# A two-layer graph network on one core: degrees turned on TensorE, four counted groups for five in layer 1, and a split by upper halves

## The chip, the cores and the metric

The kernel runs on one core of a Trainium2 chip. The metric is the device time of one execution in microseconds. A core has TensorE (PE, with its weight loads PEld), VectorE (DVE), ScalarE (ACT), GpSimd (POOL) and SyncE (SP). Each of them takes its instructions in order; they meet through semaphores. SP issues nearly all plain transfers here, POOL all gathers of rows.

## The reference

There are 12500 nodes with 256 features each, and 200000 edges, sorted by destination. `dst` is 12500 u², so that low nodes have many edges and high ones few.

```python
def _sage_conv(x, src, dst, W_l, b_l, W_r):
    msgs = x[src]
    agg = segment_sum(msgs, dst)
    deg = segment_sum(ones, dst)
    mean = agg / maximum(deg, 1.0)[:, None]
    return mean @ W_l + b_l + x @ W_r

h = relu(_sage_conv(x, src, dst, W1_l, b1, W1_r))
h = relu(_sage_conv(h, src, dst, W2_l, b2, W2_r))
out = layernorm(x + h @ W3 + b3)
```

## The kernel before, in words

**Two ways to a sum.** The edges lie in 1563 tiles of 128, the nodes in NB = 98 blocks of 128. The sums over edges are formed in one of two ways.

*Gathered.* For a tile of edges POOL gathers 128 rows of the table by an indirect DMA (`got`, L251), four tiles a round, into one of four buffers `got`. DVE makes one-hot tiles (`one` L208, `two` L214), PE multiplies each tile's rows into a strip of 32 destinations (`part_ps`, L263), ACT copies (`some`, L273), PE spreads the strips over 128 destinations (`sum_ps`, L279), and DVE adds them to a ring of eight blocks in SBUF (`sums`, L293). In layer 1 a column of ones gives the degree too (L285, added to the row `degs` at L289). POOL may start a round when the strips of four rounds ago are done.

*Counted.* For the lowest destinations, in groups of DN = 256, there is no gather. A matrix of counts (source by destination) is made by one-hot products: `pick` (DVE, L680), `low` and `aft` (DVE, L684 and L690), `count_ps` (PE, L723 and L727), copied by ACT into `counts` (L729). Then one product per group, over all 98 blocks of x, gives the sums (`dense_ps`, L655): x stands in HBM as three bf16 parts whose sum is x (`x3_d`), and its rows are loaded two blocks at a time (`rows`, L649, four buffers). In layer 1 the degrees of a counted group come from 196 products with a column of ones (L744). The first HG1 = 5 groups are counted in layer 1, HG = 7 in layer 2. Layer 2's table is h in the same three parts (`h3_d`). A group counted in layer 1 is stored to `count_d` (L778) and loaded again in layer 2; the last two counted in layer 1 simply stay in the two buffers `counts`.

`lows[g]` is the first tile that may hold a destination of group g, for g = 0 to 7: 0, 208, 304, 376, 432, 488, 536, 576. Gathers of layer 1 start at `lows[HG1]`, those of layer 2 at `lows[HG]`.

**Parts.** `exact` (L629) makes the three parts: ACT rounds to bf16, DVE subtracts, ACT rounds the rest, DVE subtracts. It runs for the 98 blocks of x (`split_rows`, in layer 1's first stage) and for the 98 blocks of h (`first_block`).

**Blocks.** When a block's sums are complete, `first_block` (L907) in layer 1, in three pieces, loads the block's rows of x, transposes them (`transposed`, L852: PE L855 into a bank of four 128-column places, ACT's copy L857 to `own_t`), and multiplies sums and rows by the weights (`sage`, L874). A mean needs the reciprocal of the degree of each node as a column (`rdeg`), while the ring holds degrees as a row of one partition (`degs`). Before, the row is stored to HBM (`deg_d`, L913) and read back as a column (L918); DVE then does the max and the reciprocal (L922, L923). `last_block` does layer 2's, in five pieces, with the last weights and the layer norm.

**What sets the order.** The order on PE and POOL is written out by hand; DVE, ACT and SP get theirs from a scheduler, in order of expected readiness. `layer` (L576) runs over the rounds of gathers: each round is one `gathers.step()`, then up to three pieces of blocks, and between these counted work from a generator. How much counted work stands in a round is set by cost: `due = dense_cost * min(1, (i + 1 - i0) / (n - i0 - 8))`, so all of it is spread evenly over the rounds of the layer, less the last eight. The costs are estimates written in the kernel (`COST_DENSE`, `count_cost` and so on), and `mixed` interleaves parts of a stage. `stages_1` gives the stages of layer 1: stage 0 counts group 0 and splits x; each later stage multiplies group g - 1, counts group g and stores. `stages_2` does the same for layer 2. By these formulas, layer 1 has 269 rounds (eight of them in the set-up), and its stages, in rounds, take 57, 40, 41, 37, 41 and 38; layer 2 has 247 rounds, and its stages take 31, 51 and five times 31.

Of the kernel before, what the change touches and what calls it, by code (L numbers as in the profile page):

```python
# [7 lines left out]
F32 = mybir.dt.float32  # L8
F16 = mybir.dt.float16
BF16 = mybir.dt.bfloat16  # L10
# [3 lines left out]
OP = mybir.AluOpType  # L14
# [9 lines left out]
P = 128  # L24
# [25 lines left out]
def by_runs(  # L50
# [27 lines left out]
    nc = tc.nc  # L78
    N, D = x.shape
    E = src.shape[0]  # L80
    NB = -(-N // P)
    NC = D // P
# [14 lines left out]
    def at_most(t):  # L97
        return N * ((t + SLACK) / NT) ** 2 + 2

    HG1, HG, DN = 5, 7, 256
    lows = [max(t for t in range(0, NT, 2 * G) if t == 0 or at_most(t) < DN * g) for g in range(HG + 1)]
    highs = [min(t for t in range(0, NT, G) if at_least(t) >= DN * (g + 1)) for g in range(HG)]
    HT = highs[-1]
# [21 lines left out]
    dram = ctx.enter_context(tc.tile_pool(name="dram", bufs=1, space=DRAM))  # L127
# [1 line left out]
    x3_d = dram.tile([P, NB, 3, D], BF16, name="x3_d")  # L129
    h3_d = dram.tile([P, NB, 3, D], BF16, name="h3_d")  # L130
    count_d = dram.tile([HG1 - 1, P, NB, DN], BF16, name="count_d")
    deg_d = dram.tile([NB, P], F32, name="deg_d")


    src_t = consts.tile([P, (CH - C0) * P], I32, name="src_t")
# [14 lines left out]
    ones = consts.tile([P, 1], F32, name="ones")  # L150
# [144 lines left out]
    with tc.tile_pool(name="setup", bufs=1) as su, \  # L295
# [163 lines left out]
        start = su.tile([P, HC], F32, name="start")  # L459
# [8 lines left out]
        for g, (c0, c1) in enumerate(spans):  # L468
            n = c1 - c0
# [46 lines left out]
        for t in range(0, HT, 32):  # L516
            n = min(32, HT - t)
# [52 lines left out]
    work = ctx.enter_context(tc.tile_pool(name="work", bufs=2))  # L570
# [57 lines left out]

    def exact(t, s, rest):  # L629

        nc.scalar.copy(s[:, 0], t)
        nc.vector.tensor_tensor(rest, t, s[:, 0], op=OP.subtract)
        nc.scalar.copy(s[:, 1], rest)
        nc.vector.tensor_tensor(s[:, 2], rest, s[:, 1], op=OP.subtract)

    def split_rows(b):
        t = load_rows(x, N, b, "split_sb")
        s = work.tile([P, 3, D], BF16, name="parts")
        exact(t, s, t)
        nc.sync.dma_start(x3_d[:, b], s)  # L640

    def product(g, table3, c_sb):
# [116 lines left out]
    def counting(g):  # L759
        return sum(count_cost(t) for t in range(lows[g], highs[g]))  # L760
# [20 lines left out]
    def loaded(g, c_sb):  # L781
        for b0 in range(0, NB, 14):
            nc.sync.dma_start(c_sb[:, b0:b0 + 14, :DN], count_d[g, :, b0:b0 + 14])
            yield 0.5

    def dense(g, table3, c_sb, waiting, with_deg):
        for p in product(g, table3, c_sb):
            if isinstance(p, float):
                yield p
            else:  # L790
                d_sb = p
        if with_deg:
            yield from degrees(g, c_sb)
        for j in range(DN // P):
            waiting.append((g * (DN // P) + j, d_sb[:, :, j * P:(j + 1) * P]))

    def splits():
        for b in range(NB):
            split_rows(b)
            yield COST_SPLIT  # L800
# [1 line left out]
    D_1 = NB * COST_DENSE + DN // P * (NB // 14) * COST_DEGREES  # L802
    D_2 = NB * COST_DENSE
    MOVED = NB // 14 * 0.5
    assert NB % 14 == 0 and HG == HG1 + 2

    def stages_1(waiting):

# [9 lines left out]

    def stages_2(waiting):

        order = [HG1 - 1, HG1, HG1 + 1, *range(HG1 - 1)]
        for i, g in enumerate(order):
            parts = [(dense(g, h3_d, counts[(HG1 - 1 + i) % 2], waiting, False), D_2)]
            if 1 <= i < HG - 1:
                n = order[i + 1]
                to = counts[(HG1 + i) % 2]
                parts.append((count(n, to), counting(n)) if n > HG1 else (loaded(n, to), MOVED))
            yield parts
# [15 lines left out]
    def load_rows(table, n_rows, b, name, tag=None):  # L844
        t = work.tile([P, D], F32, name=name, tag=tag or name)
        n = min(P, n_rows - b * P)
        if n < P:
            nc.vector.memset(t, 0.0)
        nc.sync.dma_start(t[:n], table[b * P:b * P + n, :])
        return t  # L850

    def transposed(t, ps, name):  # L852

        for c in range(NC):
            nc.tensor.transpose(ps[:, c], t[:, c * P:(c + 1) * P], ident)  # L855
        s = work.tile([P, NC, P], F32, name=name)
        copied = nc.scalar.copy(s, ps[:, :NC])  # L857
        return s, copied.ins.name

    def ring(b):  # L860

        r = (b % RB) * P
        return sums[:, :, r:r + P], degs[:, r:r + P]
# [10 lines left out]
    def sage(own_t, copied, b, agg, of_ring, wl, wr, bias, name):  # L874

        ps = block_bank()
        for c in range(NC):
            product = nc.tensor.matmul(ps[:, 0], lhsT=agg[:, c], rhs=wl[:, c], start=c == 0,  # L878
                                       stop=c == NC - 1)
            if c == 0:  # L880
                tc.add_manual_dep(product.ins, copied, LANDED, reason="the other products' rows")
        for c in range(NC):
            product = nc.tensor.matmul(ps[:, 1], lhsT=own_t[:, c], rhs=wr[:, c], start=c == 0,  # L883
                                       stop=c == NC - 1)
        if of_ring:
            zeroed = nc.scalar.copy(agg, zeros)  # L886
            tc.add_manual_dep(zeroed.ins, product.ins.name, LANDED, reason="it signals for all")
        own = work.tile([P, D], F32, name="own")
        nc.vector.tensor_add(own, ps[:, 1], bias)  # L889
        nc.vector.scalar_tensor_tensor(own, ps[:, 0], rdeg[:, b:b + 1], own, op0=OP.mult, op1=OP.add)  # L890
        h = work.tile([P, D], F32, name=name)
        nc.scalar.activation(h, own, AF.Relu)  # L892
        return h, own

    def block_bank():

        if block_pool is None:
            t = mixed_pool.tile([P, 4, P], F32, name="block_ps", tag="mixed")
        else:
            t = block_pool.tile([P, 4, P], F32, name="block_ps")  # L900
        return t.rearrange("p (two a) l -> p two (a l)", two=2)

    def turned():
        t = block_bank()
        return t.rearrange("p two (a l) -> p (two a) l", l=P)

    def first_block(b, agg=None):  # L907
        x_sb = load_rows(x, N, b, "x_sb")
        of_ring = agg is None
        if of_ring:  # L910
            overlap(b, True)
            agg, deg_row = ring(b)
            nc.sync.dma_start(deg_d[b:b + 1], deg_row)  # L913
        yield True
        if of_ring:
            deg = work.tile([P, 1], F32, name="deg")
            with nc.allow_non_contiguous_dma(reason="a row becomes a column"):
                nc.sync.dma_start(deg, deg_d[b, :, None])  # L918
        x_t, copied = transposed(x_sb, turned(), "own_t")
        yield True  # L920
        if of_ring:
            nc.vector.tensor_scalar(deg, deg, 1.0, None, op0=OP.max)  # L922
            nc.vector.reciprocal(rdeg[:, b:b + 1], deg)  # L923
        h, own = sage(x_t, copied, b, agg, of_ring, w1l_sb, w1r_sb, biases[:, 0], "h")
        if of_ring:
            nc.scalar.copy(deg_row, zeros[0:1, 0])
        nc.sync.dma_start(h_d[b * P:(b + 1) * P, :], h)
        s = work.tile([P, 3, D], BF16, name="parts")
        exact(h, s, own)
        nc.sync.dma_start(h3_d[:, b], s)  # L930
        yield True

    def last_block(b, agg=None):
        h_sb = load_rows(h_d, NB * P, b, "h_sb", "split_sb")
        of_ring = agg is None
        yield True
        if of_ring:
            overlap(b, False)
            agg, _ = ring(b)
        h_t, copied = transposed(h_sb, turned(), "own_t")  # L940
        yield True
        h2, _ = sage(h_t, copied, b, agg, of_ring, w2l_sb, w2r_sb, biases[:, 1], "h")
        x_sb = load_rows(x, N, b, "x_sb")
        yield True
        h2_t, _ = transposed(h2, turned(), "own_t")
        nc.vector.tensor_add(x_sb, x_sb, biases[:, 2])
        yield True
        y = block_bank()
        for c in range(NC):
            nc.tensor.matmul(y[:, 0], lhsT=h2_t[:, c], rhs=w3_sb[:, c], start=c == 0, stop=c == NC - 1)  # L950
        z = work.tile([P, D], F32, name="z", tag="own")
        nc.vector.tensor_add(z, y[:, 0], x_sb)
        stats = work.tile([P, 6], F32, name="stats")
        nc.vector.bn_stats(stats, z)
        mv = work.tile([P, 2], F32, name="mv")
        nc.vector.bn_aggr(mv, stats)
        std = work.tile([P, 1], F32, name="std")
        nc.scalar.activation(std, mv[:, 1:2], AF.Sqrt, bias=eps)
        rstd = work.tile([P, 1], F32, name="rstd")
        nc.vector.reciprocal(rstd, std)  # L960
        nc.vector.tensor_scalar(z, z, mv[:, 0:1], rstd, op0=OP.subtract, op1=OP.mult)
        n = min(P, N - b * P)
        nc.sync.dma_start(out[b * P:b * P + n, :], z[:n])
        yield True
# [386 lines left out]
```

## Time and profile before

| what | value |
|---|---|
| median of three runs | 2878.88 us (2876.56 to 2884.81) |
| the profiled execution's own time | 2859.28 us |
| its span, first to last instruction | 2857.5 us |
| mean granted TensorE clock | 0.918 |
| first gather starts, last gather of layer 1 ends | 24.8 us, 1532.8 us |
| first gather of layer 2 starts, last ends | 1556.8 us, 2804.6 us |
| gathers in layers 1 and 2 | 1076, 988 |
| layer 1's products by group, first matmul | 421.5, 667.7, 883.0, 1077.2, 1298.4 us |

The page gives, for each engine, the busy time, the share of the span and the number of instructions; then the span in 40 slices, a digit a slice; then the chain that ended last; then groups of instructions as "line, engine, operation, out<-in, count | busy, mean ns of one | idle before, and what ended it". Names have their numbers left out, so `h_d` stands for `h3_d` too and `x_d` for `x3_d`. "issue" is idle time in which the engine waited for nothing that the profile shows. A matmul with fp32 operands appears as two records.

### The profile page before, as it was taken

To read this page: it belongs to the slowest core of one execution; us is meant where nothing else is said; L and a number is where in the kernel's file an instruction comes from. 1 tells how busy PE (TensorE), PEld (TensorE's weight loads), DVE (VectorE), ACT (ScalarE), POOL (GpSimd) and SP (SyncE) were. 2 spreads that over 40 slices of the span, in tenths; PEclk is the share of its full clock that TensorE was granted. 3 is DMA by queue.
4 is the path that set the end of the run, shared out by engine and by line. 5 is a ranking of instruction groups with operands and counts; after the bars stand their busy time and mean duration, and the time that the engine had idled before them with its cause. 6 is when DMAs were issued, how large, how long until landed. Compare 5 with 4: busy or idle time off the path is not lost.

```text
span 2857.5 us, 53445 instructions
## 1 busy us (share of the span) xinstructions
PE 2325.8 (81%) x18268; PEld 1607.4 (56%) x18268; DVE 1461.6 (51%) x4334; ACT 1099.4 (38%) x2270; POOL 2054.2 (72%) x2074
## 2 busy tenths in 40 slices
PE   3466675888988998999996678777889889999995
PEld 1122333565755666766664455555656667777773
DVE  6688774654555565565564124443324344444443
ACT  0422774654554564565563013333112122222222
POOL 5777775677777777777675777777777777777771
PEclk9876877997998999999997999999999999999998
DMA  4466679778878879877764777777989999888872
GB/s 124 135 180 179 190 210 300 248 225 257 267 224 254 291 219 297 262 215 228 247 212 132 229 244 231 222 225 226 294 285 306 295 301 309 283 264 270 271 248 70
DMA packets 420975, 676.49 MB, mean 237 GB/s; under 512 B 72420, under 2 KB 279386, under 8 KB 420698
## 3 DMA queue, kind: packets, MB, share of 16 engines
q1 hardware_dynamic: 316263, 400.60, 43.5%
q0 software_dynamic: 99072, 270.66, 31.3%
q8 instruction: 150, 2.46, 0.4%
q10 hardware_dynamic: 5362, 1.72, 0.3%
q14 instruction: 128, 1.04, 0.1%
HBM read 582.84 MB, written 89.92 MB: 235 GB/s over the span
## 4 chain that ended last, share of the span: by engine, by line
PE 45%; DMA 24%; POOL 11%; issue 8%; DVE 7%; ACT 4%; SPq 1%; DVEq 0%; ACTq 0%; POOLq 0%
PE dense_ps L655 17%; POOL got L251 11%; PE part_ps L263 6%; PE block_ps L878 5%; DMA got<-h_d,src_t 4%; DMA rows<-h_d 4%; PE block_ps L883 4%; PE count_ps L723 4%; DMA x_sb<-in_x_dram 4%; PE sum_ps L279 4%; DMA rows<-x_d 4%; DMA split_sb<-in_x_dram 3%; DMA got<-in_x_dram,src_t 2%; PE block_ps L950 2%; PE block_ps L855 2%
## 5 line engine op out<-in xcount | busy, mean ns | idle before, releaser
L251 POOL DMA_INDIRECT got<-in_x_dram,src_t x1076 | 1109.7, 1031 | 420.3 <-issue 282.7
L251 POOL DMA_INDIRECT got<-h_d,src_t x988 | 942.4, 954 | 329.4 <-issue 260.8
L655 PE MATMUL dense_ps<-counts,rows 128*128 128x256 bf16 x7056 | 958.4, 279 | 75.4 <-DMA rows<-h_d 41.1
L655 PEld LDWEIGHTS <-rows 128*128 128x128 bf16 x7056 | 674.2, 99 | 296.7 <-issue 81.4
L729 ACT CAST counts<-count_ps 128x686 f32 (+2 forms) x620 | 540.2, 872 | 237.8 <-PE count_ps L723 188.0
L263 PE MATMUL part_ps<-got,one 128*32 128x257 f32 (+1 forms) x4128 | 359.9, 422 | 181.9 <-DMA got<-h_d,src_t 106.1
L723 PE MATMUL count_ps<-pick,low 128*128 128x490 bf16 (+2 forms) x1052 | 321.1, 359 | 62.5 <-ACT counts L729 37.2
L680 DVE TENSOR_SCALAR pick<-steps,key_t 128x686 bf16<-128x686 f16 (+2 forms) x748 | 301.0, 414 | 120.9 <-PE count_ps L723 107.3
L208 DVE TENSOR_TENSOR one<-lo_t,lane_b 128x128 f32<-128x128 bf16 x516 | 148.1, 287 | 322.5 <-PE part_ps L263 318.8
L273 ACT COPY some<-part_ps 128x257 f32<-128x257 f32 (+1 forms) x361 | 134.5, 373 | 414.2 <-PE part_ps L263 413.1
L279 PE MATMUL sum_ps<-two,some 128*128 128x128 f32 x1444 | 240.9, 293 | 39.4 <-DVE own L890 38.6
L263 PEld LDWEIGHTS part_ps<-got,one 128*32 128x32 f32 x4128 | 87.2, 112 | 299.8 <-issue 237.9
L279 PEld LDWEIGHTS sum_ps<-two,some 128*128 128x128 f32 x1444 | 209.4, 205 | 55.3 <-DVE own L890 39.9
L293 DVE TENSOR_TENSOR sums<-sums,sum_ps 128x256 f32 x361 | 148.3, 411 | 145.8 <-PE sum_ps L279 113.2
L886 ACT COPY sums<-zero 128x256 f32<-128x256 f32 x172 | 69.3, 403 | 393.4 <-PE block_ps L883 391.8
L889 DVE TENSOR_TENSOR own<-block_ps,biases 128x256 f32<-128x256 f32 x196 | 82.6, 421 | 210.3 <-PE block_ps L883 209.9
L723 PEld LDWEIGHTS <-low 128*128 128x128 bf16 x1052 | 105.0, 101 | 140.0 <-DVE pick L680 33.6
L857 ACT COPY own_t<-block_ps 128x256 f32<-128x256 f32 x294 | 108.8, 372 | 125.6 <-PE block_ps L855 124.5
L684 DVE TENSOR_TENSOR low<-low_t,lane_b 128x512 bf16<-128x512 bf16 x187 | 127.7, 683 | 39.4 <-PE count_ps L727 39.0
L892 ACT ACTIVATE h<-own 128x256 f32<-128x256 f32 x196 | 81.7, 417 | 145.3 <-DVE own L890 145.0
L727 PE MATMUL count_ps<-aft,low 128*128 128x98 bf16 x614 | 133.3, 217 | 0.0
L878 PE MATMUL block_ps<-w1l_sb,sums 128*128 128x256 f32 x352 | 114.2, 453 | 12.5 <-DVE sums L293 6.0
(177 smaller groups left out, 2417.9 us busy)
## 6 DMA issues: line engine op xcount, KB each, us to landing
rows<-h_d SPq DMA_DIRECT2D x343, 384.0 KB
rows<-x_d SPq DMA_DIRECT2D x245, 384.0 KB
count_d<-counts SPq DMA_DIRECT2D x28, 896.0 KB
counts<-count_d SPq DMA_DIRECT2D x28, 896.0 KB
x_sb<-in_x_dram SPq DMA_DIRECT2D x194, 128.0 KB
x_d<-parts SPq DMA_DIRECT2D x98, 192.0 KB
h_d<-parts SPq DMA_DIRECT2D x98, 192.0 KB
got<-in_x_dram,src_t POOLq DMA_INDIRECT x1076
```

The source lines that it names most:

```text
L208: nc.vector.tensor_tensor(one, lo[:, a:a + n * (G - 1) + 1:n].unsqueeze(2).to_broadcast([P, G, W]), lane_b[:, :W].unsqueeze(1).to_broadcas ...
L251: rows = nc.gpsimd.indirect_dma_start(out=g[:, j, :D], out_offset=None, in_=self.table, in_offset=bass.IndirectOffsetOnAxis(ap=src_t[:, e: ...
L263: strip = nc.tensor.matmul(part_ps[j * W:(j + 1) * W, :width], lhsT=one[:, j], rhs=g[:, j, :width], start=r == 0, stop=r == n - 1)
L273: nc.scalar.copy(some[:, :width], part_ps[:, :width])
L279: nc.tensor.matmul(sum_ps[:, c], lhsT=some[:, c * P:(c + 1) * P], rhs=two, start=True, stop=True)
L293: nc.vector.tensor_add(own, own, sum_ps[:, :NC])
L655: nc.tensor.matmul(ps[:, c], lhsT=rows[:, b % 2, k, c * P:(c + 1) * P], rhs=c_sb[:, b, :DN], start=False, stop=b == NB - 1 and k == 2 and ...
L680: nc.vector.tensor_scalar(r[:, :w * NB], steps[:, :w * NB], key_t[g][:, t - lo_g:t - lo_g + 1], None, op0=OP.is_equal)
L723: nc.tensor.matmul(c[:, a * NB:b * NB], lhsT=s, rhs=r[:, a * NB:b * NB], start=True, stop=alone)
L727: nc.tensor.matmul(c[:, :NB], lhsT=before[0], rhs=before[1], start=False, stop=True)
L729: nc.scalar.copy(to[:, :, bass.ds(off_act.at(t), w)], c.rearrange("p (d s) -> p s d", s=NB))
L878: product = nc.tensor.matmul(ps[:, 0], lhsT=agg[:, c], rhs=wl[:, c], start=c == 0, stop=c == NC - 1)
```

## The change

Three things change together.

The row of degrees becomes a column on PE: a product with one row of contraction (lhsT the row of degrees, rhs a single one) writes one column right behind the transposed rows of the same block, in the same bank; ACT's copy takes 257 columns and not 256, and DVE does max and reciprocal on that last column. `deg_d`, its store and its load go. The ring's overlap and the degrees move from the block's first piece to its second.

HG1 is 4 and not 5. Layer 1 multiplies four groups, and counts five of the seven. Group 4's destinations are gathered in layer 1. Layer 2 begins with groups 3 and 4, which stay in SBUF, counts groups 5 and 6, and loads groups 0, 1 and 2. By the formulas above layer 1 has 283 rounds, its stages 71, 50, 50, 46 and 50 rounds; layer 2 has 247, its stages 28, 49, 47 and four times 28 to 29.

`exact` takes the upper half of each fp32 number as its bf16 part, read in place with a stride of two, so that both subtractions of DVE come first, one after the other, and ACT copies the two upper halves after that. The first rest goes into a tile of its own for x, which shares the two buffers of `own`; the third part, on DVE, is now the first write into `parts`.

```diff
-    HG1, HG, DN = 5, 7, 256
+    HG1, HG, DN = 4, 7, 256
...
-    deg_d = dram.tile([NB, P], F32, name="deg_d")
...
     def exact(t, s, rest):
-        nc.scalar.copy(s[:, 0], t)
-        nc.vector.tensor_tensor(rest, t, s[:, 0], op=OP.subtract)
-        nc.scalar.copy(s[:, 1], rest)
-        nc.vector.tensor_tensor(s[:, 2], rest, s[:, 1], op=OP.subtract)
+        def upper(a):
+            return a.bitcast(BF16).rearrange("p (n h) -> p n h", h=2)[:, :, 1]
+
+        nc.vector.tensor_tensor(rest, t, upper(t), op=OP.subtract)
+        nc.vector.tensor_tensor(s[:, 2], rest, upper(rest), op=OP.subtract)
+        nc.scalar.copy(s[:, 0], upper(t))
+        nc.scalar.copy(s[:, 1], upper(rest))

     def split_rows(b):
         t = load_rows(x, N, b, "split_sb")
         s = work.tile([P, 3, D], BF16, name="parts")
-        exact(t, s, t)
+        exact(t, s, work.tile([P, D], F32, name="rest", tag="own"))
...
-        order = [HG1 - 1, HG1, HG1 + 1, *range(HG1 - 1)]
+        order = [*range(HG1 - 1, HG), *range(HG1 - 1)]
...
-    def transposed(t, ps, name):
+    def transposed(t, ps, name, more=0):
         for c in range(NC):
             nc.tensor.transpose(ps[:, c], t[:, c * P:(c + 1) * P], ident)
-        s = work.tile([P, NC, P], F32, name=name)
-        copied = nc.scalar.copy(s, ps[:, :NC])
-        return s, copied.ins.name
+        s = work.tile([P, NC * P + 1], F32, name=name)
+        n = NC * P + more
+        copied = nc.scalar.copy(s[:, :n], ps.rearrange("p c l -> p (c l)")[:, :n])
+        return s[:, :NC * P].rearrange("p (c l) -> p c l", l=P), s[:, NC * P:], copied.ins.name
...
     def first_block(b, agg=None):
         x_sb = load_rows(x, N, b, "x_sb")
         of_ring = agg is None
+        yield True
+        ps = turned()
         if of_ring:
             overlap(b, True)
             agg, deg_row = ring(b)
-            nc.sync.dma_start(deg_d[b:b + 1], deg_row)
-        yield True
-        if of_ring:
-            deg = work.tile([P, 1], F32, name="deg")
-            with nc.allow_non_contiguous_dma(reason="a row becomes a column"):
-                nc.sync.dma_start(deg, deg_d[b, :, None])
-        x_t, copied = transposed(x_sb, turned(), "own_t")
-        yield True
+            nc.tensor.matmul(ps[:, NC, 0:1], lhsT=deg_row, rhs=ones[0:1, 0:1], start=True, stop=True)
+        x_t, deg, copied = transposed(x_sb, ps, "own_t", int(of_ring))
         if of_ring:
             nc.vector.tensor_scalar(deg, deg, 1.0, None, op0=OP.max)
             nc.vector.reciprocal(rdeg[:, b:b + 1], deg)
+        yield True
         h, own = sage(x_t, copied, b, agg, of_ring, w1l_sb, w1r_sb, biases[:, 0], "h")
```

More of the change, by code (lines that the diff above doesn't have):

```diff
@@ L804, in by_runs @@
     MOVED = NB // 14 * 0.5
-    assert NB % 14 == 0 and HG == HG1 + 2
+    assert NB % 14 == 0 and HG > HG1
     def stages_1(waiting):
@@ L939, in last_block @@
             agg, _ = ring(b)
-        h_t, copied = transposed(h_sb, turned(), "own_t")
+        h_t, _, copied = transposed(h_sb, turned(), "own_t")
         yield True
@@ L944, in last_block @@
         yield True
-        h2_t, _ = transposed(h2, turned(), "own_t")
+        h2_t, _, _ = transposed(h2, turned(), "own_t")
         nc.vector.tensor_add(x_sb, x_sb, biases[:, 2])
```

## The prediction

> **What bounds the kernel now.** I read the page first. PE is busiest, but GpSimd (POOL) holds 7 tenths in nearly every slice, across two layers that differ in all else:
>
> ```profile
> PE 2325.8 (81%) x18268; PEld 1607.4 (56%) x18268; DVE 1461.6 (51%) x4334; ACT 1099.4 (38%) x2270; POOL 2054.2 (72%) x2074
> ...
> POOL 5777775677777777777675777777777777777771
> ...
> L251 POOL DMA_INDIRECT got<-in_x_dram,src_t x1076 | 1109.7, 1031 | 420.3 <-issue 282.7
> L251 POOL DMA_INDIRECT got<-h_d,src_t x988 | 942.4, 954 | 329.4 <-issue 260.8
> ```
>
> The reader is to see that the idle time before a gather is mostly "issue", which waits for nothing: about 0.3 us each. One gather costs (942.4 + 329.4) / 988 = 1.29 us with the layer boundary in it. A level 72% is thus a full engine.
>
> Second, the waits of POOL in layer 1, to the boundary:
>
> ```profile
> POOL got L251 <- issue: 276.0, 905, 0.6
> POOL got L251 <- PE part_ps L263: 64.0, 37, 11.8
> POOL got L251 <- DMA h_d<-parts: 24.0, 1, 24.0
> POOL got L251 <- PE count_ps L727: 22.0, 14, 18.1
> ```
>
> Real waits (over 1.5 us, gather by gather) come to 64 us: 8 before 160 us, 39 from 459 to 545 us, 17 later. In layer 2 the only one besides the 24 us boundary is 2.6 us.
>
> Third, windows by stage (PE, PEld, DVE, ACT, POOL busy, clock, DMA share, GB/s):
>
> ```profile
> 71.00:421.00 350.00, 216.90 (x1149) 96.14 (x1150) 275.60 (x778) 171.21 (x347) 266.14 (x244) 0.76 0.60 177
> 421.00:570.00 149.00, 104.21 (x813) 68.62 (x813) 86.08 (x255) 82.09 (x170) 85.38 (x84) 0.85 0.86 276
> 570.00:1533.00 963.00, 868.04 (x7554) 616.82 (x7553) 547.54 (x1633) 525.33 (x980) 721.68 (x717) 0.94 0.78 243
> 1557.00:1985.00 428.00, 326.06 (x2503) 225.14 (x2504) 144.06 (x406) 116.31 (x203) 325.04 (x339) 0.92 0.73 224
> 1985.00:2303.00 318.00, 276.85 (x2200) 201.69 (x2197) 107.50 (x323) 56.73 (x157) 240.53 (x254) 0.95 0.91 296
> 2303.00:2779.00 476.00, 449.87 (x3627) 343.86 (x3630) 213.85 (x655) 115.67 (x326) 357.14 (x377) 0.99 0.86 278
> ```
>
> Layer 2 issues a gather each 1.25 to 1.26 us to its end, though PE reaches 95%. The dip is 421 to 570 us, 84 gathers in 149 us. The timeline says why:
>
> ```profile
> 454.87 0.93 PEld L279 LDWEIGHTS sum_ps<-two,some 128*128 128x128 f32 x4 [23.75 <-DVE own L890]
> ...
> 459.45 1.05 POOL L251 DMA_INDIRECT got<-in_x_dram,src_t  x1 [18.07 <-PE count_ps L727]
> ```
>
> PE stood 23.5 us behind one block's DVE instruction (L890); DVE had stood behind the splits of x, which end at 524 us, 100 us after stage 1 began. Four gather buffers then ran full, and POOL stopped. So POOL is the bound, interrupted once by late splits.
>
> **What the skill says.** The Trainium skill, "Perfetto Trace Analysis", Identifying the Most-Contended Engine: a PE's busy share is a poor measure, occupancy is fair for GpSimd. The trace agrees: PE at 95% leaves the gathers undisturbed. "GPSIMD Engine Reference", 1. Specifications: its SBUF interfaces are shared with VectorE, which contends in some modes. Agrees: a gather took 1093 ns mean at 71 to 421 us, where DVE is 79% busy, 1007 ns at 570 to 1533 us (57%), 950 ns at 2303 to 2779 us (45%). "DMA: Bandwidth & Descriptors", Anatomy of one DMA: some 2 us per transfer are fixed, mostly completion. Agrees: at the boundary `deg_d` was issued at 1532.11 us and its read-back at 1534.11 us, when it had landed.
>
> **The change, part by part.** Sum against the profiled execution (2859.28 us, span 2857.5). The three runs' median is 19.6 us above; I add the difference to the median.
>
> *Degrees.* Goes: 88 stores and 88 loads of 0.5 KB. SP was held 148.3 + 13.3 us (L913, for DVE) and 36.0 us (L918, for the store), and queued behind it were loads of rows and blocks; DVE was held 69.2 us (L922, 46 times). Comes: 90 K=1 products into the transposes' bank. No row has one; the one-row product L285 took 0.15 to 0.23 us, so with two passes 0.15 to 0.5 us, 14 to 45 us of PE; I take 0.25, 22 us. The copy L857 reads one column more of 256 (372 ns): nothing. New wait: PE, in order, stands at that product until DVE has added the degrees (L289, in one block of eight L871 too), and dense products and strips queue behind it; DVE's max then waits for ACT's copy where it waited for a DMA. Cover: the queued gathers (four buffers, 5 us each) and PE's slack after the next edit. Without cover 90 times about 0.5 us, 45 us. On the path: 0. Boundary: 24 us of POOL idle hold one deg round trip, of 2 us. I take -2.
>
> *Four counted groups.* The lower bound of gathered tiles goes from 488 to 432: 56 more gathers, 14 rounds. Price: layer 1 late, (722.4 busy + 241.4 idle - 29.9 for PE) / 717 = 1.30 us; 56 x 1.30 = **+73 us on POOL**. Bounds 1.25 to 1.44 us (layer 2; the DVE-laden stretch): +70 to +81. Nothing can hide it, POOL being full.
> Layer 1 loses one product (588 matmuls, 79 us busy, some 68 alone on PE), 196 degree columns (5 us), the count of group 5 (72 tiles; the 68 of group 6 take 33 us of PE: 35), 49 loads of 384 KB and 7 stores of 896 KB. It gains 14 rounds of strips and 7 sums, 13 us of PE. So 95 us less, near a tenth. Stage costs by the planner: 840.9 units over 253 rounds become 713.9 over 267, 20% fewer per round; stage 0 gets 71 rounds for 57, so its 98 splits have 25% more time. In the changed order the last split stands behind 240 picks, not 279 (group 0 has 236): splits end with their stage. So I take 48 of the later 56 us of stalls as gone: **-48 us**. Bounds 20 and 56.
> Layer 2 gets count 5 (35 us of PE, a gather about 30 ns longer over 47 rounds: +6 us; layer 1 loses the same) and one load of counts less. Its last four products get 28.7 rounds each for 31.4. At 2464 to 2779 us PE did 150 us of work in 157; of it 67 is dense, so 28.7 rounds need 67 + 83 x 28.7 / 31.4 = 143 of 144 us. DMA, at 0.91 where counts are loaded, also gets 6% denser. The first half has room. Excess 3 to 8 us a stage, less what four buffers cover: **+8 us**, bounds 0 to +40.
>
> *Halves.* A split was ACT, DVE, ACT, DVE (0.40 + 0.42 + 0.40 + 0.43 us with hand-overs: 1.75); now both subtractions come first and the copies follow: some 0.5 to 0.8 us less for each of 98 splits and 98 blocks. It helps stage 0 alone, and is in the 48. The waits for the load (87.0 us) and for the parts' stores (18.3 + 15.6 us) move from ACT to DVE; picks and one-hot tiles queue behind, and PE for these. Their cover is stage 0's 25%; without it some 40 us come back. `rest` shares the two buffers of `own`, so DVE can also wait for ACT's second copy, 0.4 us: hidden likewise.
>
> Sum: -2 + 73 - 48 + 8 = **+31 us**: span 2888, median 2878.88 + 31 = 2910.
>
> **Rivals.** *All stalls go, layer 2 hides the rest (same):* -2 + 73 - 64 + 0 = +7, or 2886. For it: layer 2's undisturbed gathers at 95% PE. Against: 8 of the 64 us lie in the set-up, which isn't touched.
> *Gathers get shorter (faster):* layer 1's mean of 1031 ns is 77 above layer 2's, through DVE. Were half of it to go with fewer picks per round, 1132 x 0.038 = 43 us go too: 31 - 43 = -12, or 2867. It decides from 35 ns on (40 us, under the 0.3% bound). Against: set-up and splits stay, and only count 5, a share of some 6 us, leaves.
> *PE takes POOL's place, or DVE's new DMA waits renew the stall (slower still):* 20 of 48 us regained and +25 in layer 2: -2 + 73 - 20 + 25 = +76, or 2955; with either alone, about 2925 to 2940. For it: the 143 of 144 us, DMA at 0.91. Against: PE there keeps 7 us idle a stage unasked.
> *The change doesn't do what it says:* that the SP waits go but cost nothing before. I hold this true of the degrees, and it's in the forecast.
>
> **How the numbers follow.** What a measurement can tell from no change is 0.3%, 8.6 us: below 2870 faster, above 2887.5 slower. Forecast (2892 to 2930) 0.57; same 0.12; faster 0.11; slower still 0.20. Part of "same" reaches over its bound: faster 0.11, same 0.11, slower 0.78. The range leaves out most of "faster" and the far end of "slower still": 2878 to 2945.
>
> **What would show it.** 1132 + 988 gathers; last of layer 1 ending 20 to 30 us later than 1532.8; no POOL wait over 5 us at 400 to 600 us; layer 1 at 1.30 to 1.35 us a gather with PE well under 90%; layer 2 at 1.26 to 1.28 us, PE at 97% in its last 400 us. Wrong if the gathers of layer 1 fall below 1.0 us mean, if the dip stays, or if layer 2 passes 1.30 us.

## The result, and the profile after

The changed kernel takes 2921.48 us (2915.51 to 2924.63) where the kernel before took 2880.12 in the same comparison: a ratio of 1.014, 95% interval 1.0118 to 1.0162. It is slower by 41 us; 2910 (2892 to 2930) had been forecast.

Its page, lines as those shown of before:

```profile
PE 2334.3 (80%) x17810; PEld 1595.9 (55%) x17810; DVE 1470.1 (50%) x4373; ACT 1106.8 (38%) x2282; POOL 2131.2 (73%) x2130
...
POOL 5777877777777777777775777777777776677771
...
L250 POOL DMA_INDIRECT got<-in_x_dram,src_t x1132 | 1178.1, 1041 | 371.8 <-issue 300.3
L250 POOL DMA_INDIRECT got<-h_d,src_t x988 | 950.9, 962 | 356.2 <-issue 260.6
```

POOL's instructions grew by 56 gathers, and its busy time by 77 us, while PE's stayed. In layer 1 less idle time stands before more gathers (371.8 us for 420.3), so stalls have gone; in layer 2 more stands before the same 988 (356.2 for 329.4). The sixes in POOL's row, near its end, are new.

POOL's waits in layer 1, 60 to 1553 us, of the changed kernel:

```profile
POOL got L250 <- issue: 293.6, 963, 0.3
POOL got L250 <- DMA got<-in_x_dram,src_t: 16.8, 55, 0.3
POOL got L250 <- PE part_ps L262: 7.6, 13, 2.3
```

The 64.0 us behind PE have become 7.6, and the longest wait is 2.3 us where it was 18.1 (the line of L727).

Windows of the changed kernel (columns as before; the first two stretches are the same times as those shown of before, the others end at its own boundaries):

```profile
71.00:421.00 350.00, 207.03 (x1054) 94.57 (x1053) 248.59 (x711) 141.17 (x303) 273.82 (x239) 0.75 0.59 177
421.00:570.00 149.00, 112.99 (x721) 63.55 (x722) 94.85 (x284) 86.92 (x182) 115.77 (x110) 0.78 0.80 249
570.00:1553.00 983.00, 845.14 (x7070) 590.27 (x7069) 527.83 (x1609) 490.27 (x958) 752.90 (x755) 0.93 0.71 224
1577.00:2224.00 647.00, 515.31 (x3967) 356.78 (x3968) 260.60 (x720) 220.95 (x374) 492.23 (x507) 0.93 0.70 221
2224.00:2838.00 614.00, 569.63 (x4574) 434.73 (x4577) 253.83 (x770) 136.47 (x384) 442.04 (x465) 0.98 0.85 282
```

The dip at 421 to 570 us is gone, 110 gathers for 84. From 570 us layer 1 takes 983 / 755 = 1.30 us a gather, with PE at 86% and not 90%. Most of the loss is in the last row, the last four products of layer 2: 465 gathers in 614 us are 1.32 us each, where layer 2 had given one each 1.26 us to its end. PE did no more there than before. Here are the last 400 us before the last product ends, of the kernel before and then of the changed one:

```profile
2379.00:2779.00 400.00, 378.77 (x3061) 289.00 (x3064) 178.43 (x547) 97.03 (x273) 299.77 (x317) 0.99 0.85 275
2438.00:2838.00 400.00, 378.23 (x3055) 290.65 (x3057) 173.81 (x527) 93.08 (x263) 287.67 (x302) 0.99 0.83 275
```

PE is busy for 378 us of 400 in both, 94.6%, but beside 302 gathers and not 317. In all ten profiles that are not from slow chips it is 375 to 381 us, beside 301 to 319 gathers. So what looked like room at 95% was little or none. The timeline shows POOL held by PE at work, not by a stopped PE:

```profile
2527.09 0.82 PE L658 MATMUL dense_ps<-counts,rows 128*128 128x256 bf16 x6
2527.74 0.61 PE L278 MATMUL sum_ps<-two,some 128*128 128x128 f32 x4
2528.19 0.82 PE L658 MATMUL dense_ps<-counts,rows 128*128 128x256 bf16 x6
2528.94 0.64 PE L262 MATMUL part_ps<-got,one 128*32 128x256 f32 x8
...
2529.88 0.95 POOL L250 DMA_INDIRECT got<-h_d,src_t  x1 [3.79 <-PE part_ps L262]
```

A dense product, a sum, a dense product and the strips follow one another; the gather had to wait for these strips, 3.79 us in all.

Where the time lies, by profile (us; "waits" are the idle times of POOL over 0.35 us inside a layer, added up from the trace's gathers; "again" is the first run below):

| profile | span | layer 1: first gather to end of last | its waits | mean gather, ns | layer 2: first gather to end of last | its waits | after the last gather |
|---|---|---|---|---|---|---|---|
| before | 2857.5 | 1508.0 | 80 | 1031 | 1247.8 | 7 | 52.9 |
| before, again | 2889.0 | 1523.0 | 84 | 1043 | 1261.1 | 22 | 55.2 |
| changed | 2919.1 | 1526.6 | 5 | 1041 | 1282.3 | 39 | 59.3 |

Against the mean of the two profiles of before, layer 1 took 11 us more, layer 2 28 us more and the tail 5 us more: 44 us, near the 41 us of the medians.

### The profile page after: what moved, and what is told of

It reads as the page before. It is cut to its first block, busy times and chain, and to the rows that moved or that the text cites. A ratio compares the mean times of both kernels' runs of the same rounds, so it can differ in the third digit from the quotient of the medians.

```text
span 2919.1 us, 52104 instructions
## 1 busy us (share of the span) xinstructions
PE 2334.3 (80%) x17810; PEld 1595.9 (55%) x17810; DVE 1470.1 (50%) x4373; ACT 1106.8 (38%) x2282; POOL 2131.2 (73%) x2130
## 3 DMA queue, kind: packets, MB, share of 16 engines
q14 instruction: 125, 1.02, 0.1%
## 4 chain that ended last, share of the span: by engine, by line
PE 35%; DMA 20%; POOL 19%; issue 11%; DVE 2%; ACT 1%; DVEq 0%; SPq 0%; ACTq 0%; POOLq 0%
POOL got L250 19%; PE dense_ps L658 12%; DMA got<-in_x_dram,src_t 8%; DMA got<-h_d,src_t 5%; PE part_ps L262 5%; PE block_ps L882 4%; PE block_ps L887 3%; DMA rows<-h_d 3%; DMA x_sb<-in_x_dram 3%; PE sum_ps L278 2%; PE count_ps L726 2%; PE block_ps L951 2%; PE block_ps L858 2%; DMA rows<-x_d 1%; DVE own L894 0%
## 5 line engine op out<-in xcount | busy, mean ns | idle before, releaser
L250 POOL DMA_INDIRECT got<-in_x_dram,src_t x1132 | 1178.1, 1041 | 371.8 <-issue 300.3
L250 POOL DMA_INDIRECT got<-h_d,src_t x988 | 950.9, 962 | 356.2 <-issue 260.6
L658 PE MATMUL dense_ps<-counts,rows 128*128 128x256 bf16 x6468 | 874.2, 278 | 36.0 <-DMA rows<-h_d 25.0
L658 PEld LDWEIGHTS <-rows 128*128 128x128 bf16 x6468 | 618.1, 99 | 238.0 <-issue 81.5
L262 PE MATMUL part_ps<-got,one 128*32 128x257 f32 (+1 forms) x4240 | 377.4, 429 | 353.4 <-DMA got<-in_x_dram,src_t 208.6
L262 PEld LDWEIGHTS part_ps<-got,one 128*32 128x32 f32 x4240 | 93.2, 112 | 474.5 <-issue 381.4
L890 ACT COPY sums<-zero 128x256 f32<-128x256 f32 x174 | 70.2, 404 | 447.8 <-PE block_ps L887 447.7
L861 ACT COPY own_t<-block_ps 128x256 f32<-128x256 f32 (+1 forms) x294 | 109.4, 373 | 121.6 <-PE block_ps L858 119.2
L882 PE MATMUL block_ps<-w1l_sb,sums 128*128 128x256 f32 x360 | 124.2, 476 | 1.7 <-DVE sums L292 1.2
```

Of the source, the lines that this page charges most:

```text
L250: rows = nc.gpsimd.indirect_dma_start(out=g[:, j, :D], out_offset=None, in_=self.table, in_offset=bass.IndirectOffsetOnAxis(ap=src_t[:, e: ...
L262: strip = nc.tensor.matmul(part_ps[j * W:(j + 1) * W, :width], lhsT=one[:, j], rhs=g[:, j, :width], start=r == 0, stop=r == n - 1)
L658: nc.tensor.matmul(ps[:, c], lhsT=rows[:, b % 2, k, c * P:(c + 1) * P], rhs=c_sb[:, b, :DN], start=False, stop=b == NB - 1 and k == 2 and ...
```

## The experiments

Each time is a median on its own chip, with the kernel before run beside it; ratios are what can be compared across them.

**The kernel before, unchanged.**

> The kernel before, unchanged, for a second profile of it: the first profiled execution (2859.28 us) was 20.8 us faster than the median of its runs (2880.12), while the changed kernel's profiled execution stood at its median. Theory: the 20 us lie in layer 1, where PE, granted less clock, holds the gathers for longer, so a second profile near 2880 us shows more than 64 us of POOL waiting for PE in layer 1, and layer 2 as in the first (1248 us from first to last gather). Rival: they lie in the gathers themselves, whose mean in layer 1 is then over 1031 ns by some 18 ns.

2885.72 us, ratio 1.0014 (0.9993 to 1.0035). The profile, 2890.83 us, is at the upper end of its runs (2873 to 2894). Neither theory holds alone. Waits in layer 1 are nearly the same (84 for 80 us); 12 us lie in longer gathers (1043 for 1031 ns), 13 us in layer 2, chiefly waits. So two profiles of one kernel differ by 31 us, spread over both layers, and the prediction's sum had been made against the faster.

**Four groups alone.**

```diff
-    HG1, HG, DN = 5, 7, 256
+    HG1, HG, DN = 4, 7, 256
```

> The kernel before with HG1 = 4 alone; degrees and split as before. Theory (POOL full; the stretched first stage and the sparser counted work per round remove the stalls of layer 1): the whole change is this edit, 2910 to 2930 us, and no POOL wait over 5 us at 400 to 600 us. Rival (the halves removed the stalls): the dip stays, and the time is 2945 to 2965 us.

2925.33 us, ratio 1.0161 (1.0119 to 1.0204): within the error, this one edit takes as long as the whole change. But the stall did not go entirely. Waits in layer 1 fell from 80 to 30 us, and one stop remained, far over the 5 us of the theory:

```profile
526.08 1.22 PE L279 MATMUL sum_ps<-two,some 128*128 128x128 f32 x4 [24.59 <-DVE own L890]
530.21 0.94 POOL L251 DMA_INDIRECT got<-in_x_dram,src_t  x1 [16.34 <-PE part_ps L263]
```

It is the stop shown of before, again behind L890, 70 us later. The longer first stage did not bring the splits to its end: they ended at 579 us, when stage 1 had run since 490 us, a lag of 89 us where it had been 103. In DVE's order the last split stood behind 269 picks, not 279; stage 0 has 236. The rest of the waits went with this edit all the same. Whether the longer stage or the sparser counted work after it did that, this run can't tell.

**The halves alone.**

```diff
-        nc.scalar.copy(s[:, 0], t)
-        nc.vector.tensor_tensor(rest, t, s[:, 0], op=OP.subtract)
-        nc.scalar.copy(s[:, 1], rest)
-        nc.vector.tensor_tensor(s[:, 2], rest, s[:, 1], op=OP.subtract)
+        nc.vector.tensor_tensor(rest, t, upper(t), op=OP.subtract)
+        nc.vector.tensor_tensor(s[:, 2], rest, upper(rest), op=OP.subtract)
+        nc.scalar.copy(s[:, 0], upper(t))
+        nc.scalar.copy(s[:, 1], upper(rest))
```

> The kernel before with the split by halves alone. Theory: a split takes some 0.5 us less, the dip at 420 to 570 us shrinks by a part, 2860 to 2880 us. Rival (the halves removed the stalls): 2835 to 2850 us, the whole 39 us of the dip. Third: waits for DMA now stand on DVE and renew the stall, over 2885 us.

2851.26 us, ratio 0.9899 (0.9867 to 0.9932): 29 us faster, better than the theory and a microsecond short of the rival's stretch. Its profile is of the fastest of its five runs (2835.95 us). The splits end at 443 us, with their stage (stage 1 begins at 442), and not at 524 or 543, though the stage has its old 57 rounds; the last one stands behind 238 picks. No stop over 5.1 us is left. What DVE waited for at the splits, from 70 to 545 us, in the kernel before and then with the halves:

```profile
DVE split_sb L632 <- ACT parts L631: 57.0, 49, 4.4
DVE parts L634 <- ACT parts L633: 14.8, 16, 6.2
```

```profile
DVE rest L635 <- DMA split_sb<-in_x_dram: 15.8, 19, 2.0
DVE parts L636 <- DMA x_d<-parts: 7.5, 11, 2.2
DVE rest L635 <- ACT parts L638: 6.2, 1, 6.2
```

Before, DVE stood some 70 us behind ACT's roundings (and ACT behind the loads); with the halves it waits some 30 us. The timeline of one split:

```profile
442.42 0.40 ACT L637 COPY parts<-split_sb 128x256 bf16<-128x256 bf16 x1 [0.37 <-DMA split_sb<-in_x_dram]
442.93 0.41 DVE L635 TENSOR_TENSOR rest<-split_sb 128x256 f32<-128x256 f32 x1
443.37 0.41 ACT L638 COPY parts<-rest 128x256 bf16<-128x256 bf16 x1 [0.54 <-DVE rest L635]
443.52 0.40 DVE L636 TENSOR_TENSOR parts<-rest 128x256 bf16<-128x256 f32 x1
443.99 0.32 SPq L644 DMA_DIRECT2D x_d<-parts  x1
```

ACT's first copy needs no DVE, and DVE's second subtraction needs no ACT. From the first subtraction to the end of the last of the four it is 1.0 us (442.93 to 443.92), where the four had taken 1.75.

**The degrees alone.**

> The kernel before with the K=1 product for the degrees alone; five groups and the split as before. Theory: nothing on the path, 2872 to 2888 us, whatever SP no longer waits for. Rival (SP's 198 us and DVE's 69 us of waits did hold loads back and PE with them): below 2865 us. Other rival (PE stands at the K=1 product for the sums of degrees): above 2895 us.

2883.38 us, ratio 1.0008 (0.9989 to 1.0028): nothing, as the theory had it. The K=1 product (one row of contraction) and what its engine waited for before it, in that run:

```profile
L915 PE MATMUL block_ps<-ones,degs x176: 245/266/368, 124.1 to 1563.6; 1*128 1x1 f32 x176
...
  DVE degs L871: 9.0, 11
  DVE degs L288: 6.1, 8
```

88 products are 176 records with a median of 266 ns, and PE stood 15 us for the sums of degrees over the whole layer. POOL's waits in layer 1 are no shorter in this profile (103 us for 80 and 84), so the transfers and SP's waits that went had held nothing on the path.

**Degrees and halves, five groups.**

> The changed kernel with five counted groups again (HG1 = 5), so degrees and halves without the third edit. Theory (the halves alone gave 2851 us, the degrees alone nothing, the groups cost): 2845 to 2860 us. Rival (degrees and halves hinder each other, both putting waits on DVE): over 2870 us.

2850.99 us, ratio 0.987 (0.9815 to 0.9925). So without the change of groups the other two edits make the kernel faster, and all of that is the halves'. Against this kernel the third edit, four groups for five, costs 2.7% by the ratios; by profile, 37 us in layer 1 (1489.8 to 1526.6), 31 us in layer 2 (1251.6 to 1282.3) and 2 us in the tail.

**48 gathers more that add nothing.**

```diff
-    C0 = lows[HG1] // P
+    FROM = lows[HG1] - 48
+    C0 = FROM // P
...
-    groups = [(t, 2) for t in range(lows[HG1], PAIRS, 2 * G)] + [(t, 1) for t in range(PAIRS, NT, G)]
+    groups = [(t, 2) for t in range(FROM, PAIRS, 2 * G)] + [(t, 1) for t in range(PAIRS, NT, G)]
```

> The changed kernel with its gathers of layer 1 beginning 48 tiles earlier: 12 more rounds, 48 more gathers, of edges that are counted anyway and add nothing. Theory (POOL is full, nothing hides a gather): 48 x 1.30 = 62 us more than the changed kernel, less some DVE interference, 2970 to 2990 us. Rival (gathers lie partly beside PE's work): under 2950 us.

2972.41 us, ratio 1.0299 (1.025 to 1.0349), 51 us more than the changed kernel (each on its chip), at the lower end of the theory. By profile layer 1 grew by 42 us: 48 gathers of 1.02 us with a pause of 0.31 us each make 64 us, less 20 us because the other 1132 were 18 ns shorter on average (1023 for 1041 ns), less 2 us of waits. So the gathers are exposed, at 0.9 to 1.1 us each. That this is under 1.30 is not clear of the noise: the two ratios differ by 46 us, give or take 16, and two profiles of the kernel before differ by 12 ns in the mean gather.

**Layer 2 paced otherwise.** The planner costs layer 2's counting at half, so that its last four products get 32 rounds each and not 28.7. The work is the same.

```diff
-                parts.append((count(n, to), counting(n)) if n > HG1 else (loaded(n, to), MOVED))
+                parts.append(((c / 2 for c in count(n, to)), counting(n) / 2) if n > HG1
+                             else (loaded(n, to), MOVED))
```

> The changed kernel with the counting in layer 2 costed at half for the planner, so that layer 2's two counting stages take 38 rounds each and its last four products 32 each, as many as before the change. The work is the same. Theory (layer 2's 34 us are PE's, packed too tightly in the last four products): 2888 to 2902 us, and POOL's waits for PE in layer 2 fall from 39 to some 6 to 15 us. Rival (denser transfers, or the change in the blocks): 2912 us or more.

2873.40 us, ratio 0.9955 (0.9929 to 0.9982): a larger gain than forecast, and with it the changed kernel is 0.5% faster than the kernel before. POOL's waits from 1600 to 2810 us, of the changed kernel, and then of this one:

```profile
POOL got L250 <- issue: 244.4, 800, 0.6
POOL got L250 <- PE part_ps L262: 43.5, 47, 3.9
```

```profile
POOL got L250 <- issue: 249.5, 819, 0.3
POOL got L250 <- PE part_ps L262: 13.9, 25, 5.4
```

By profile layer 2 fell from 1282.3 to 1252.8 us, the tail from 59.3 to 48.4 and layer 1 by 4 us, which the edit doesn't touch. So the time that layer 2 lost came from where the planner put the work, not from its amount. The edit thins the transfers of the last four products too, but these do not explain the loss: PE waited for rows there for 23 us before the change (26 in the second profile) and for 24 us after it. With the pacing it is 14 us, so up to 10 us of the gain may be theirs.

**Six groups.**

```diff
-    HG1, HG, DN = 4, 7, 256
+    HG1, HG, DN = 6, 7, 256
```

> The changed kernel with six counted groups in layer 1 (48 gathers fewer than five groups, one product more). Theory (POOL sheds 62 us, but PE, at 90% in layer 1, gets 95 us more and takes its place): 2850 to 2890 us with over 60 us of POOL waiting for PE in layer 1. Rival (POOL alone decides): 2790 to 2810 us.

2909.97 us, ratio 1.0085 (1.0061 to 1.011): slower than either theory, and for the reason of the first: PE. POOL's waits from 60 to 1500 us, and the window from its first product to the end of the layer:

```profile
POOL got L250 <- issue: 237.2, 776, 0.6
POOL got L250 <- PE part_ps L262: 191.1, 117, 8.5
```

```profile
428.00:1578.00 1150.00, 1068.23 (x9462) 764.98 (x9459) 662.50 (x1921) 658.73 (x1161) 781.50 (x783) 0.98 0.78 252
```

PE is at 93% and POOL waits 191 us for it. With degrees and halves in all three, five groups (0.987 of the kernel before) beat four (1.014) and six (1.0085): five lie near the point where the two engines balance; one group less fills POOL, one more fills PE.

**Three kernels on two slow chips.** These ran where every kernel, the one before too, took 16% longer: the three on one chip (the kernel before: 3358 us), the repeat of the last on another (3359 us). First, the kernel before with only stage 0 stretched to 71 rounds:

```diff
-    COST_DENSE, COST_DEGREES, COST_SPLIT = 0.7, 1.6, 0.8
+    COST_DENSE, COST_DEGREES, COST_SPLIT = 0.7, 1.6, 2.08
```

> The kernel before with the splits of x costed higher for the planner, so that layer 1's first stage takes 71 rounds, as in the changed kernel, and not 57; nothing else. Theory (more rounds for the splits alone remove the dip, as the prediction had it): no POOL wait over 5 us at 400 to 600 us; PE is packed 8% tighter in the later stages, which gives some back: 2845 to 2880 us. Rival (it takes the shorter chain of the halves, or the sparser later stages): the dip stays at over 25 us, 2880 to 2910 us.

Then degrees and halves with five groups and layer 2 paced as above (the changed kernel with that edit, and `HG1, HG, DN = 5, 7, 256`):

> Degrees and halves with five counted groups, with the counting in layer 2 at half cost for the planner. Theory (layer 2's POOL waits for PE only 10 us with five groups, so there is little to win): 2838 to 2852 us. Rival (the pacing of layer 2 is worth what it was worth with four groups, 48 us): under 2820 us.

And the same with the count of the sixth group in layer 2's first stage, twice:

```diff
-            parts = [(count(g, counts[g % 2]), counting(g))]
+            parts = [(count(g, counts[g % 2]), counting(g))] if g < HG1 else []
...
-            if 1 <= i < HG - 1:
+            if i < HG - 1:
...
-                parts.append(((c / 2 for c in count(n, to)), counting(n) / 2) if n > HG1
+                parts.append(((c / 2 for c in count(n, to)), counting(n) / 2) if n >= HG1
```

> As the one with five groups and half cost, and the count of the sixth group moves from layer 1's last stage into layer 2's first: 35 us of PE leave layer 1, where POOL still waits 45 us for PE, for the part of layer 2 where PE has room. Theory: 15 to 25 us of layer 1's POOL waits go, layer 2 gives 6 us back: 2822 to 2840 us, the fastest of all. Rival (the moved count packs layer 2 too tightly again, or layer 1's waits aren't PE's load): 2850 us or more.

> The same kernel as the moved count of the sixth group, once more, because the chip on which it and its two neighbours ran was 16% slower with every kernel. Theory, on a chip where the kernel before takes about 2880 us: 2822 to 2840 us, with layer 1's POOL waits for PE at 10 to 25 us where degrees and halves alone had 45. Rival (the moved count wins nothing): 2845 to 2855 us.

3331.30 us (0.9916, 0.989 to 0.9943), 3319.40 (0.9882, 0.985 to 0.9915), 3320.53 (0.9882, 0.9848 to 0.9917) and 3330.87 (0.9924, 0.99 to 0.9947). None of their expectations can be judged, since POOL is not the bound there. POOL's waits of the first, over its whole span ("remote" is a release whose source the trace doesn't tell):

```profile
POOL got L251 <- issue: 517.1, 1687, 1.0
POOL got L251 <- PE part_ps L263: 265.1, 113, 11.4
POOL got L251 <- remote: 195.3, 113, 3.6
```

A gather took 1036 ns in layer 1, as elsewhere, but POOL waited hundreds of microseconds in both layers. Why is open. The granted TensorE clock was lower in all these runs (0.87 to 0.89, where the other chips had 0.90 to 0.93), but by too little for 16%. One thing can be read even here: in the first of these kernels, with its stage 0 of 71 rounds, the splits ended at 627 us, 79 us after stage 1 had begun, much as with four groups alone. Of the kernels that ran on other chips the fastest are the halves with five groups, with the degrees turned on PE or without: 2851 us.

## Why the prediction was right, and where it was not

**POOL is the bound; 56 gathers go on the path.** Right, and so was the price of +73. Layer 1 without its waits (what exceeds the usual 0.3 us before a gather) took 1433 to 1456 us in the five profiles with five groups and 1510 to 1523 us in the three with four: 71 us between the means, 1.27 us for each of the 56. The 48 gathers that add nothing gave less, 0.9 to 1.1 us each, with the error named there. By its busy share POOL looked a quarter empty (77% from 570 us to the end of layer 1); the pause of 0.3 us before each gather is the rest, so its occupancy, which the prediction took for a fair measure, was none here.

**48 us of stalls go.** More went: the waits of POOL inside layer 1 fell from 80 and 84 to 5 us, by 69 us if only what exceeds 0.3 us is counted. That lies above the bound of 56, and some of it came from the set-up, which I had left out. The cause was half wrong. I had put it on the rounds given to stage 0 and had let the halves help. But the splits end with their stage (within 6 us) in every kernel with the halves, with 57 rounds or 71, and some 80 to 110 us late in every kernel without them, with 71 rounds too. The 240 picks before the last split, which I had counted under the four groups, are the halves' work: 238 with the halves alone, 269 with four groups alone. What four groups alone do is to shrink the waits that the late splits cause: 30 us are left, a stop of 16 us among them. The halves alone leave 35 us (45 with the degrees) and no such stop. Each does most of the work without the other, so together they save far less than their sum; that is why the halves are worth 29 us alone and nearly nothing beside four groups (1.014 with them and with the degrees, 1.0161 without). That the rounds of stage 0 by themselves, without sparser work later, would shrink the dip was tried and not settled.

**Degrees, on the path 0.** Right, by the run of this edit alone; a product took 0.42 us of PE where I took 0.25, inside the bounds. (The one-row product L285, from which I had this, takes 0.22 to 0.27 us in the trace, not 0.15 to 0.23.) The 2 us at the layer boundary were wrong: POOL's wait there was 24.0 and 25.1 us before and is 24.7 us.

**The halves' waits move to DVE and are hidden.** Right that they move and cost nothing: DVE waited 19.9 us for the loads and some 9 us for the stores. Wrong that they need the longer stage as cover, without which some 40 us would come back: with 57 rounds nothing came back, because the waits for ACT that went (some 70 us) were more than those that came. There may be a small price: gathers were 1046 to 1048 ns in layer 1 with the halves and five groups, 1028 to 1043 without, which is little more than two profiles of one kernel differ by.

**Layer 2, +8 (0 to +40).** This is the term that was mis-sized. Layer 2 took 28 us more than the mean of the two profiles of before, and the tail 5 us more. Some 20 of the 28 are waits; the other 8 are gathers that became longer (962 for 954 ns), which had been put at 6 and set against a like gain in layer 1. The work was foreseen rightly: 143 us of PE in a stage, and the last four have 142 on average. But I had compared it with 144 us of gathers and let four buffers cover the rest, because PE at 95% seemed to leave room. Before, PE had kept 7 to 17 us idle in each of the last four products (17, 13, 7 and 7), in short waits for rows and for ACT and DVE. It kept as much after (19, 14, 7 and 5). The 570 us of work in the four and the 43 us that PE had kept idle before make 613 us, and the four took 614 (157, 156, 151 and 150), where their 464 gathers at 1.26 us would have taken some 585. That the packing is the cause is shown by the other pacing, with the same work: 40 us came back in layer 2 and the tail by profile, 48 in the whole by the medians, up to 10 of them perhaps through the transfers.

**+31, 2910.** The size of the whole owes something to luck, since two errors partly cancel. Against the mean of the two profiles of before, layer 1 took 11 us more where +25 had been forecast, because more stalls went; layer 2 and the tail took 33 us more where +8 had been forecast. And the sum was made against a profile that was 20 us faster than the median. Of the signs that had been named, layer 2's 1.26 to 1.28 us a gather and PE's 97% in its last 400 us did not come: it was 1.30 us (1282.3 us for 988 gathers), at the edge of what was to count as wrong, and 94.6%. Of the rivals, the one with PE in POOL's place came true in layer 2 alone, near the +25 that it had there.

## What to carry to other kernels

Where one engine is full in nearly every slice, price a change by what it puts on that engine, and count stalls that go as gains only once: two edits that cure the same stall don't add up. Where work is spread by a planner's costs, moving a stage changes how tightly everything after it is packed, and this can cost as much as the work that was moved; read a stage's need as its busy time plus the idle time that it kept before (here 570 + 43 us for four products, and 614 measured). An engine at 95% may have no room: look whether that share stays when the work beside it changes. Take more than one profile before making a sum against it, when executions differ by 1%.

## What the runs showed of the hardware

- A product with one row of contraction and one column is not small to PE: two records of 266 ns (median), which overlap: 37.9 us busy for the 90 of the changed kernel, or 0.42 us each. The four strips of a round, 257 columns each, took 0.64 us.
- GpSimd's gathers last longer where DVE works more: 950 ns in layer 2's last stages, 1023 to 1050 ns in layer 1. In the changed kernel's trace the 441 gathers with no DVE instruction beside them took 948 ns on average, the other 1679 took 1019. Which instructions do it is not shown: the 94 beside a split's first subtraction were 393 ns longer than 950, but nearly all of them lay beside other DVE work too, and the 7 that did not were no longer at all; of those beside `pick` all 642 were 126 ns longer, the 79 beside nothing else 26 ns. A longer gather also meets more instructions, so such averages overstate.
- PE was busy for 375 to 381 of the last 400 us of products in all ten profiles that are not from slow chips, whether POOL waited for it or not: its share doesn't tell whether it is the bound.
- Two profiles of one kernel on chips with nearly the same median (2880 and 2879 us) differed by 31 us in span.
- Two chips ran everything 16% slower (3358 and 3359 us for some 2880), with gathers of the usual length. Whether it is the chips, or the time at which they were used, is not shown.
